# Two layers of banded products: three norm columns on GpSimd, a band copy on ScalarE alone, and a new order of operations in both layers

## The chip, the cores and the metric

The kernel runs on one NeuronCore of one Trainium2 chip. Its engines are TensorE (PE in the profile, with its weight loads as PEld), VectorE (DVE), ScalarE (ACT), GpSimd (POOL) and SyncE (SP), which issues almost all of the DMA transfers. The metric is the time of one execution in device microseconds; the profile's span is the time from the first to the last instruction, a little shorter.

## The reference

The input x is a 512 x 512 grid of 64 channels in 32-bit floating point. Two layers of the same form follow each other, each with its own weights:

```python
x = x + conv(gn(x))            # twice
# gn: group norm, 32 groups of 2 channels over the whole grid
# conv:
xn    = ln(x)                                        # over 64 channels
left  = (xn @ Wl + bl) * mask * sigmoid(xn @ Wlg + blg)   # 64 -> 128
right = (xn @ Wr + br) * mask * sigmoid(xn @ Wrg + brg)
gate  = sigmoid(xn @ Wog + bog)
out[i, j, h] = sum over d = -4..4 of left[i + d, i, h] * right[i + d, j, h]
return (ln(out) * gate) @ Wo + bo                    # 128 -> 64
```

So of `left` only a band of nine entries for each row is ever used, `right` and `gate` are needed on the whole grid, and `out` mixes nine neighbouring rows of `right` for each of the 128 hidden channels. The group norm of layer two needs sums over the whole output of layer one.

## The kernel before

The rows are cut into nine overlapping blocks of 64 (56 new rows each), the columns of a block into two chunks of 128 for each half of the grid: 18 chunks a layer. The two halves of the grid lie on the two halves of the 128 partitions. A chunk is handled in 16 steps (`NU`), each of one unit of eight columns, and the function `layer` runs over the steps. In one step t several units are in different stages, so that the engines overlap:

- Loading (`load`, `fetch`, `take_left`, `recall`; all on SP at the start of a step): z, a unit of the input; XR, the input again for the residual; A, a slab of the left band (8 slabs in a chunk, 4 transfers each, in three buffers); zg, a stored transposed unit, loaded for step t + 2 into one of two buffers.
- Input norms: `scaled` and `moved` (z times ga, plus gb; on GpSimd except early in a layer; in every fourth step also the units of the next step, "scale next" and "move next"), `inner_stats` (VectorE), `centred` and `rescaled` (GpSimd, for the unit of step t + 2), `transposed` (TensorE, for t + 1), `kept` (ScalarE copies the transposed unit to zT, SP stores it as "later").
- The right product: `right` twice (32 TensorE matmuls each for columns 0 to 3 and 4 to 7, into pairs of PSUM banks), `right_gate` (ScalarE sigmoid into sg), `right_end` (VectorE product into RO).
- The band: `mix` is one band product of eight hidden channels, A times RO (32 matmuls in two PSUM banks). A chunk has 16, in its steps 0 to 9 as 2, 1, 2, 2, 1, 2, 1, 2, 2, 1. Each leaves two halves, which are copied back into RO: "copy a" by ScalarE; "copy b" by VectorE, except that the second band's "copy b" in layer one is ScalarE's (`SECOND_ON_ACT`).
- The output norm: `out_stats` (VectorE, 3 to 7 a step), `solve` in every fourth step ("a": three small ScalarE instructions; "d": 14 small VectorE instructions that give rs and nm for both norms), `norm` (one instruction for each of eight columns into the single buffer on: columns 0 to 3, then the rest on ScalarE, and the last `NV` on GpSimd, "norm columns").
- The output: `gates` (TensorE, zg times the gate's weights), `gated` (ScalarE sigmoid), `turned` (16 TensorE transposes of on), `times_gate` (VectorE, two products into ZH), `end` (32 matmuls with Wo, for the unit of the step before; "last product" in the lists), `ended` (VectorE adds XR; SP stores two halves), and in layer one `biased` (GpSimd adds the biases to XR) and `sums` (TensorE, the group sums for layer two).

The lists `FIRST` and `SECOND` give the order in which the operations of one step are written out for layer one and layer two. Every engine runs its own instructions in exactly that order (`InOrder`), so that a list fixes five queues at once; between engines only data and buffers make an instruction wait. PSUM buffers are handed out in rotation: four single banks in layer two (three in layer one) for gates, turned, end and solve (and the band in layer two), and two pairs of banks for the right products and the transposes (and the band in layer one). A transposed unit therefore waits until VectorE has read the first right product of the same step, and the next step's first right product until VectorE has read the second.

Below, "step 0" to "step 15" are the steps of a chunk (t modulo 16): bands in 0 to 9, solves in 0, 4, 8 and 12.

Of the kernel before, what the change touches and what calls it, by code (L numbers as in the profile page):

```python
# [31 lines left out]
UP = (1024.0 / 27.0) ** 2  # L32

APART = (False, True)
NV = (1, 2)
SECOND_ON_ACT = (True, False)

FIRST = [
    ("out stats", 2), "gates", "gated", ("project", 0), ("project", 4), "turn",
    ("sigmoid", 0), ("out stats", 3), "scale", ("right", 0), ("sigmoid", 4),  # L40
    ("norm", (0, 4)), "norm columns", "centre", "move", "last product", ("right", 4),
    "times gate", "rescale", "transpose", ("out stats", 99), "inner stats", "keep", "solve",
    "end", ("band", 0), ("copy a", 0), "sums", "bias", ("band", 1), ("copy b", 0),
    ("solve on", "a"), "scale next", "move next", ("norm", (4, 8)), ("copy a", 1),
    ("solve on", "d"), ("copy b", 1),
]
SECOND = [
    ("out stats", 3), "scale", ("out stats", 2), "gates", ("project", 0), "gated",
    ("sigmoid", 0), ("project", 4), ("out stats", 99), ("right", 0), ("sigmoid", 4), "turn",
    ("norm", (0, 4)), "last product", "norm columns", "centre", "scale next", "rescale",  # L50
    "times gate", "transpose", ("band", 0), "keep", "move next", "end", ("right", 4),
    ("copy b", 0), "inner stats", "solve", "move", ("copy a", 0), ("band", 1),
    ("solve on", "a"), ("copy b", 1), ("copy a", 1), ("norm", (4, 8)), ("solve on", "d"),
]
ORDERS = (FIRST, SECOND)

# [47 lines left out]
def tile_two_banded_layers(  # L104
# [679 lines left out]
    def layer(src: bass.AP, dst: bass.AP, w: dict, stats: bool, then=None):  # L784
# [59 lines left out]
        A, sti, sto = {}, {}, None  # L844
        order, nv, second_on_act = (x[0 if stats else 1] for x in (ORDERS, NV, SECOND_ON_ACT))
        for t in range(min(loads), last_t + 3):
# [263 lines left out]
```

## Time and profile before

| | us |
|---|---|
| median of 3 runs | 4771.6 (4764.16 to 4789.46) |
| the profiled execution | 4769.15 |
| its span | 4767.2 |
| busy DVE / PE / ACT / POOL | 4007.1 / 3885.2 / 3608.6 / 3274.7 |
| busy 2700 to 4500 us (layer two's middle): DVE / PE / ACT / POOL | 1603.7 / 1557.5 / 1468.5 / 1368.6 |

Layer one's steps with output run from 510 to 2540 us, layer two's from 2793 to the end; before each, the first units are normed and the left band is made. The operations are recorded under one source line, so that groups have to be told apart by their tiles: `bank<-zg,pack` are the gate products, `banks<-pack,zT` the right products, `bank<-ident,on` the turn, `bank<-pack,ZH` the last product, `RO<-bank` a band copy, `on<-RO,rs,nm` a norm column. In a timeline a line has the start, the length and the engine of a run of equal instructions, and in brackets how long the engine was idle before it and what ended that. A wait for several things is put down to the one that came last in the profile.

### The profile page before, as it was taken

Reading aid. Unit: us, or ns where it says so; the run is one execution under the profiler, and the core shown is the slowest. Engines: PE = TensorE matmul, PEld = TensorE weight load, DVE = VectorE, ACT = ScalarE, POOL = GpSimd, SP = SyncE. Lnnn points to the kernel's source line nnn. Section 1 sums busy time; section 2 is a strip of 40 time slices with the busy share of each in tenths; the row PEclk is TensorE's granted clock in tenths of the full one; section 3 lists DMA queues with packets and bytes.
Section 4 is the critical chain, followed back from the end, with each engine's and each line's share of the span. In section 5 each row is a group of like instructions: output and inputs, shape, how many; then the busy total and the mean of one; then the engine's idle time right before and its main releaser. Section 6 shows DMA issues by size and latency. Waiting matters only on the chain. (4 is left out here: it accounts for less than half of the span.)

```text
span 4767.2 us, 193179 instructions
## 1 busy us (share of the span) xinstructions
PE 3885.2 (81%) x76306; PEld 3337.2 (70%) x76306; DVE 4007.1 (84%) x10943; ACT 3608.6 (76%) x8410; POOL 3274.7 (69%) x3427
## 2 busy tenths in 40 slices
PE   1035899999999999999985478888888888888898
PEld 0024787888787878887864467777777777777776
DVE  7864888888888888888877488988899998999898
ACT  0023888888888888898974378888888888888887
POOL 0036888888888888888723487777777777777751
PEclk9987999999999999999997799999999999999999
DMA  7958677777777777777764867777777777777776
GB/s 311 401 120 126 182 208 204 212 217 211 212 208 208 210 208 209 214 212 210 207 171 110 104 189 208 214 220 208 210 221 214 221 212 211 213 219 215 217 200 185
DMA packets 1437809, 983.48 MB, mean 206 GB/s; under 512 B 167363, under 2 KB 1284585, under 8 KB 1432553
## 3 DMA queue, kind: packets, MB, share of 16 engines
q1 hardware_dynamic: 1432064, 969.69, 74.4%
q8 instruction: 604, 9.90, 0.9%
q14 instruction: 301, 2.46, 0.2%
q10 hardware_dynamic: 4840, 1.43, 0.1%
HBM read 658.35 MB, written 312.40 MB: 204 GB/s over the span
## 5 line engine op out<-in xcount | busy, mean ns | idle before, releaser
L381 ACT ACTIVATE on<-RO,nm,rs 128x128 f32<-128x128 f32 x3744 | 1588.5, 492 | 91.8 <-DVE nm L381 44.9
L381 PEld LDWEIGHTS banks<-pack,zT 64*128 64x128 f32 x18576 | 1304.4, 203 | 380.6 <-ACT zT L381 204.4
L381 PE MATMUL banks<-pack,zT 64*128 64x128 f32 x18576 | 1350.8, 292 | 174.4 <-ACT zT L381 149.3
L381 DVE TENSOR_TENSOR RO<-banks,sg 128x512 f32<-128x512 f32 (+1 forms) x1188 | 796.3, 677 | 464.4 <-ACT sg L381 387.6
L381 POOL TENSOR_SCALAR on<-RO,rs,nm 128x128 f32<-128x128 f32 x864 | 383.9, 451 | 975.7 <-ACT sg L381 504.5
L381 ACT ACTIVATE sg<-banks 128x512 f32<-128x512 f32 (+1 forms) x1188 | 695.0, 590 | 311.1 <-PE banks L381 287.1
L381 PE MATMUL bank<-zg,pack 64*128 64x448 f32 (+1 forms) x2304 | 727.3, 615 | 213.5 <-DMA zg<-later 193.8
L381 DVE BATCH_NORM_STATS2 sto<-RO 128x6 f32<-128x256 f32 x2304 | 803.8, 412 | 0.8
L381 DVE SCALAR_TENSOR_TENSOR ZH<-bank,pack,gate 128x448 f32<-128x448 f32 (+1 forms) x1152 | 739.5, 684 | 63.0 <-ACT gate L381 34.1
L381 ACT ACTIVATE gate<-bank 128x448 f32<-128x448 f32 (+1 forms) x1152 | 563.8, 541 | 172.6 <-issue 103.0
L381 POOL TENSOR_TENSOR z<-z,ga 128x512 f32<-128x512 f32 x536 | 681.2, 1279 | 17.2 <-DMA z<-mid_x 8.7
L381 PE MATMUL bank<-pack,ZH 128*64 128x64 f32 x18432 | 667.3, 226 | 17.8 <-DVE nm L381 16.7
L381 POOL TENSOR_TENSOR z<-z,gb 128x512 f32<-128x512 f32 x536 | 677.5, 1277 | 5.1
L381 POOL TENSOR_TENSOR z<-z,rs 128x512 f32<-128x512 f32 x586 | 618.3, 1056 | 71.6 <-DVE rs L381 44.6
L381 POOL TENSOR_TENSOR z<-z,sti 128x512 f32<-128x512 f32 x586 | 624.3, 1066 | 20.8 <-DVE sti L381 20.8
L381 PEld LDWEIGHTS bank<-pack,ZH 128*64 128x64 f32 x18432 | 587.4, 138 | 60.9 <-DVE nm L381 24.2
L381 ACT ACTIVATE zT<-banks 128x512 f32<-128x512 f32 (+1 forms) x1084 | 460.1, 475 | 72.0 <-PE banks L381 62.8
L381 DVE BATCH_NORM_STATS2 sti<-z 128x6 f32<-128x128 f32 x2344 | 504.1, 282 | 0.5 <-POOL z L381 0.3
L381 PE MATMUL bank<-ident,on 64*128 64x64 f32 x9216 | 453.8, 227 | 27.5 <-ACT gate L381 25.0
L381 PEld LDWEIGHTS bank<-zg,pack 64*128 64x128 f32 x2304 | 240.5, 191 | 336.5 <-DMA zg<-later 62.7
L381 PEld LDWEIGHTS bank<-ident,on 64*128 64x128 f32 x9216 | 426.5, 141 | 69.6 <-ACT gate L381 44.7
L381 DVE TENSOR_TENSOR XR<-bank,XR 120x512 f32<-120x512 f32 (+1 forms) x576 | 390.9, 679 | 2.5 <-PE bank L381 1.2
(154 smaller groups left out, 4020.5 us busy)
## 6 DMA issues: line engine op xcount, KB each, us to landing
later<-zT SPq DMA_DIRECT2D x576, 256.0 KB
A<-left_of SPq DMA_DIRECT2D x1152, 128.0 KB
zg<-later SPq DMA_DIRECT2D x576, 256.0 KB
z<-in_x_dram SPq DMA_DIRECT2D x576, 128.0 KB
z<-mid_x SPq DMA_DIRECT2D x576, 128.0 KB
gn_x<-in_x_dram SPq DMA_DIRECT2D x16, 4096.0 KB
XR<-in_x_dram SPq DMA_DIRECT2D x448, 112.0 KB
mid_x<-XR SPq DMA_DIRECT2D x448, 112.0 KB
```

The lines of the kernel that those rows point to most:

```text
L381: return lambda *a, **k: tc.keep_in_program_order(f(*a, **k))
```

## The change

Nothing that is computed changes. In layer two `NV` goes from 2 to 3: three of the eight norm columns are GpSimd's, five ScalarE's. In layer two `SECOND_ON_ACT` becomes true: both halves of a step's second band are copied by ScalarE. Both lists are written anew:

```diff
-NV = (1, 2)
-SECOND_ON_ACT = (True, False)
+NV = (1, 3)
+SECOND_ON_ACT = (True, True)
 
 FIRST = [
-    ("out stats", 2), "gates", "gated", ("project", 0), ("project", 4), "turn",
-    ("sigmoid", 0), ("out stats", 3), "scale", ("right", 0), ("sigmoid", 4),
-    ("norm", (0, 4)), "norm columns", "centre", "move", "last product", ("right", 4),
-    "times gate", "rescale", "transpose", ("out stats", 99), "inner stats", "keep", "solve",
-    "end", ("band", 0), ("copy a", 0), "sums", "bias", ("band", 1), ("copy b", 0),
-    ("solve on", "a"), "scale next", "move next", ("norm", (4, 8)), ("copy a", 1),
-    ("solve on", "d"), ("copy b", 1),
+    ("out stats", 2), "gates", "scale", "centre", ("project", 0), "gated", "scale next",
+    ("project", 4), "turn", ("out stats", 3), ("sigmoid", 0), "rescale", "last product",
+    ("sigmoid", 4), ("out stats", 99), ("right", 0), "transpose", ("right", 4),
+    "times gate", "inner stats", "end", ("band", 0), ("norm", (0, 4)), "solve", "sums",
+    "keep", ("copy a", 0), ("solve on", "a"), ("norm", (4, 8)), "norm columns", ("band", 1),
+    "move next", ("copy b", 0), ("solve on", "d"), "move", ("copy a", 1), "bias",
+    ("copy b", 1),
 ]
 SECOND = [
-    ("out stats", 3), "scale", ("out stats", 2), "gates", ("project", 0), "gated",
-    ("sigmoid", 0), ("project", 4), ("out stats", 99), ("right", 0), ("sigmoid", 4), "turn",
-    ("norm", (0, 4)), "last product", "norm columns", "centre", "scale next", "rescale",
-    "times gate", "transpose", ("band", 0), "keep", "move next", "end", ("right", 4),
-    ("copy b", 0), "inner stats", "solve", "move", ("copy a", 0), ("band", 1),
-    ("solve on", "a"), ("copy b", 1), ("copy a", 1), ("norm", (4, 8)), ("solve on", "d"),
+    "centre", ("out stats", 3), "gates", ("project", 0), "scale", "gated", ("out stats", 2),
+    ("project", 4), "scale next", ("sigmoid", 0), "turn", ("right", 0), "times gate",
+    ("out stats", 99), ("sigmoid", 4), "rescale", "last product", "end", "transpose",
+    ("band", 0), ("band", 1), ("right", 4), ("norm", (0, 4)), "keep", ("copy b", 0),
+    ("copy a", 0), "inner stats", ("norm", (4, 8)), "norm columns", "solve", "move next",
+    "move", ("solve on", "a"), ("solve on", "d"), ("copy a", 1), ("copy b", 1),
 ]
```

Read engine by engine, this is what becomes of the queues of one step:

| queue | before | after |
|---|---|---|
| layer one, PE and ACT | | the same order |
| layer one, DVE | out stats 5, right 0, right 4, times gate, other out stats, inner stats, end, copy b 0, solve d | other out stats directly after the first five |
| layer one, POOL | scale, norm columns, centre, move, rescale, bias, scale next, move next | scale, centre, scale next, rescale, norm columns, move next, move, bias |
| layer two, PE | | the same order |
| layer two, ACT | gated, sigmoids, norm 0 to 3, keep, copy a 0, solve a, copy a 1, norm 4 and 5 | gated, sigmoids, norm 0 to 3, keep, copy a 0, norm 4, solve a, copy a 1, copy b 1 |
| layer two, DVE | all out stats, right 0, times gate, end, right 4, copy b 0, inner stats, copy b 1, solve d | out stats 5, right 0, times gate, other out stats, end, right 4, copy b 0, inner stats, solve d |
| layer two, POOL | scale, norm columns (2), centre, scale next, rescale, move next, move | centre, scale, scale next, rescale, norm columns (3), move next, move |
| both layers, SP after the loads | store of zT ("later"), stores of the output | stores of the output, store of zT |

## The prediction

> **What bounds the kernel now.** I read the page's busy shares first, then the waits of layer two's middle (2700 to 4500 us), then the timelines of TensorE, VectorE and the SP queue beside each other.
>
> ```profile
> PE 3885.2 (81%) x76306; PEld 3337.2 (70%) x76306; DVE 4007.1 (84%) x10943; ACT 3608.6 (76%) x8410; POOL 3274.7 (69%) x3427
> ```
>
> No engine is full. VectorE (DVE) leads, and it is what the change relieves; were it the bound, the change would pay. The waits say what it waits for:
>
> ```profile
> POOL on L381 <- ACT sg L381: 320.7, 148, 7.2
> DVE RO L381 <- ACT sg L381: 119.9, 80, 9.6
> PE bank L381 <- DMA zg<-later: 115.1, 57, 4.4
> PEld bank L381 <- DMA zg<-later: 59.0, 26, 4.5
> ```
>
> Columns: total us, times, longest. The last two are one cause: the gate products wait for zg, the block recalled from DRAM. The first two follow from it. TensorE and VectorE around one such wait (step 7 of a chunk):
>
> ```profile
> 3311.59 1.15 PE L381 MATMUL bank<-RO,A 64*64 64x128 f32 x32
> 3316.83 1.86 PE L381 MATMUL bank<-zg,pack 64*128 64x448 f32 x4 [4.09 <-DMA zg<-later]
> 3318.46 3.65 PE L381 MATMUL banks<-pack,zT 64*128 64x128 f32 x32
> ```
> ```profile
> 3314.59 1.39 DVE L381 BATCH_NORM_STATS2 sto<-RO 128x6 f32<-128x256 f32 x4
> 3321.13 0.69 DVE L381 TENSOR_TENSOR RO<-banks,sg 128x512 f32<-128x512 f32 x1 [5.14 <-ACT sg L381]
> ```
>
> All engines stop, and TensorE is then slow: the same four gate products take 1.02 us one step later, the projections 1.95. Why zg is late stands in the SP queue:
>
> ```profile
> 3302.74 0.55 SPq L381 DMA_DIRECT2D zg<-later  x1
> 3303.39 0.55 SPq L381 DMA_DIRECT2D later<-zT  x1
> 3304.03 1.11 SPq L381 DMA_DIRECT2D out_dram<-XR  x2
> 3305.24 3.28 SPq L381 DMA_DIRECT2D z<-mid_x  x4
> 3308.57 1.02 SPq L381 DMA_DIRECT2D XR<-mid_x  x2
> 3309.69 3.82 SPq L381 DMA_DIRECT2D A<-left_of  x4
> 3313.61 0.55 SPq L381 DMA_DIRECT2D zg<-later  x1
> 3314.26 0.55 SPq L381 DMA_DIRECT2D later<-zT  x1
> ```
>
> SP issues back to back, some 0.55 us and a gap of 0.1 for each transfer, and without waiting: 10.9 us from recall to recall, where TensorE's two-band step takes 6.8. The zg for this step was issued at 3313.61 and the product starts 3.2 us after. So SP is the bound here. Its group for a step costs about 4.7 us, and 3 to 4 more with a slab A; slabs fall in 8 of 16 steps, all in steps 1 to 11. Taking the starts of the gate products from the timeline for 14 chunks of each layer, a chunk lasts 116.4 us (layer one) and 114.0 (layer two). Steps 0 to 3 hardly vary (7.28, 7.65, 6.86, 6.83 in layer two); steps 4 to 12 vary by up to 4 us; the shortest of each step sum to 102.6 us in layer two, 110.4 in layer one. The difference, 11.4 and 6.0 us a chunk, is waiting for SP and the slow clock after it:
>
> ```profile
> 3310.00:3330.00 20.00, 15.91 (x300) 13.91 (x299) 13.41 (x32) 12.91 (x29) 13.46 (x15) 0.83 0.81 219
> 3392.00:3412.00 20.00, 19.20 (x430) 17.40 (x429) 19.70 (x52) 17.91 (x41) 17.43 (x19) 1.00 0.78 216
> ```
>
> Columns after the length: busy PE, weight loads, DVE, ACT, POOL, then granted clock (0.83 against 1.00), DMA share, GB/s. SP waits for compute again only in steps 12 to 15 (at step 13: recall issued 3366.10, next store 3370.31). A chunk is therefore SP's unbroken run from step 15 to step 12 of the next chunk, some 95 us with the landing, and about 20 us of compute in steps 12 to 15. **Compute counts only in those 20 us, in the last 140 us of the kernel, and in the filling of the layers.**
>
> **The change part by part.** The profiled execution took 4769.15 us (span 4767.2), 2.4 below the median of 4771.6; the sum is made against it. There are 18 chunks a layer; first and last overlap filling and draining, so I count 17.
>
> Layer two, second band's copy from DVE to ACT: six a chunk, 108. Starts of successive DVE instructions lie 0.60 us apart (row 683 ns), so 65 us leave DVE; on ACT the same form costs 584 ns, 0.49 apart, 53 us. The six steps are 0, 2, 3, 5, 7 and 8, all in SP's run; in steps 2 and 3 TensorE has no idle and 6.82 us of work, so it covers DVE there as well. Effect 0. If both covers were gone, -65.
>
> Layer two, third norm column: 288 leave ACT at 0.41 us (four in 1.68), 118 us, and cost GpSimd 0.43 each (two in 0.88), 124 us. GpSimd's whole step is up to two or three pairs of scale and move (1.25 each), centre and rescale (1.02 each) and the columns (1.3). In the old order the columns wait early in the step for the turn (the 320.7 us above) with all else behind them. In the new one centre, scale, scale next and rescale are done while the turn is awaited, and only the moves are queued behind. From one norm to the next I get 5.8 us (step 0 to 1), 7.05 (2 to 3), 8.3 (3 to 4, 7 to 8), 7.05 (4 to 5), against steps of 6.8 to 9.4: columns finish at most 4.3 us after the turn, and the next turn comes over 5 us after. Rescale waits for the solve's rs after steps 0, 4, 8 and 12 as before, 7 us ahead of its transposes. Effect 0; if that slack were gone, 1.5 us at the two long intervals, 17 x 3.0 = +51.
>
> Layer two, solve: ACT now does its last norm column ahead of the solve's preparation. Behind it stand the DVE roots, then next step's right product, which frees the banks of the transposes. In steps 0, 4 and 8 SP's run covers it. In step 12 nothing does: zT starts 3362.74, preparation 3363.47, DVE's first root 3364.18 after 0.67 of waiting. One column later: +0.41 x 17 = +7; 0 to +9.
>
> Layer two, stores: out (VectorE) now precedes later (zT) in SP. At steps 14 and 15 XR's sum ends about 0.4 us before zT (3375.91 plus 0.68 against about 3377.0), so SP starts its run some 0.3 earlier: -5; bounds -7 and +2.
>
> Layer one, stores: the same swap, but here the sum ends after zT (later issued at 1803.67, out at 1804.95 once XR's sum ended at 1804.9). The later store now waits behind out: about +0.45 a chunk, +8; bounds 0 and +12.
>
> Layer one, GpSimd: its column and the bias move behind rescale; the bias is last. The bias of step t-1 must be in before VectorE's sum in t; the worst is step 4 (three moves, bias): 6.5 us after its turn, where that sum comes some 10 after. Effect 0. Below: TensorE's waits put down to GpSimd's column there (19.9 and 16.6 us in 1500, 12.9 chunks) are 2.8 a chunk, and 20 of 116 us are open: -8. Above: one column's 0.45 a chunk in the open part, +8. The sixth and seventh out-stats of steps 12 and 0 move ahead of the right product, where VectorE waits 4.35 and 0.70 us anyway; 0, bounds -6 and +6.
>
> Engine orders that the lists leave as they were: TensorE in both layers, ACT in layer one.
>
> Clock: the stall at step 12 grows slightly when VectorE is quicker, so the slow clock after it is met more often. Steps 12 to 14 average 6.19, 6.77 and 5.88 us, with worst values of 7.50, 7.42 and 6.64. I take 0.3 of the 2.7 us between, +5; bounds 0 and +46.
>
> Draining of layer two: without unit loads SP is lighter, DVE busy 36.3 of 40 us in the banded part (4626 to 4666), and late steps are ACT's six columns and two gates, 3.25 us. Some of six copies (0.60) and some eight columns (0.41): -5; bounds -7 and 0. Filling: SP issues left_of stores there; 0, bounds -5 and +5.
>
> Sum: 7 - 5 + 8 + 5 - 5 = +10, so 4779 against the profiled run, 4781 on the median's footing. I say 4780.
>
> A rule against this reading: the Trainium skill, DMA: Bandwidth & Descriptors, section Issuing engines are not separate DMA queues, says that the time a sequencer takes to initiate a DMA is usually small relative to the DMA itself. The row above has SP issuing without a break while engines wait. By the rule SP would not be the bound, DVE would be, and the sum would be that of the first rival.
>
> **The rivals.** First, VectorE is the bound after all: 84% busy overall, and layer two windows of 19.70 in 20 us speak for it; the stalls of 4 us with SP continuous speak against. It gives -65 - 5 + 15 = -55, on the median's footing (as the next two) 4717. Second, the slow clock: with a shorter compute each chunk of layer two falls into the slow form of steps 12 to 14; 17 x 2.7 = 46, and the other terms +5: 4823. It decides over 24 us from 1.1 us a chunk (19 of its own). Rows for it: step 14 is either 5.0 or 6.5, the granted clock 0.80 between 3355 and 3377; against it: the stall is already long in most chunks. Third, GpSimd becomes the bound in layer two as costed: +51 + 10, 4833; that it is busy for only 1368.6 of the 1800 us from 2700 speaks against.
>
> **How the numbers follow.** Chance of the forecast (within 0.5%, 24 us, about what a measurement of this kernel can tell from no change) 0.50. VectorE rival 0.20, faster by over 0.5%. Clock 0.16, GpSimd or an unseen wait 0.14, slower. The range leaves out the lower half of the first rival and the far end of the last: 4725 to 4830; the likeliest case's own is 4760 to 4793.
>
> **What would show it.** Right: layer two's chunk near 114 us, DVE's busy time down by about 74 us (108 x 683 ns) without a shorter span; ACT's norm columns 288 fewer, GpSimd's 288 more; more DMA zg waits, SP continuous from step 15 to 12. Wrong: chunks of 110 us or less with fewer zg waits (VectorE was the bound), or SP waiting within steps 1 to 10, or TensorE's turn waiting for GpSimd's on. Wrong altogether if SP's issue time itself changes, since every chunk rests on it.

## The result and the profile after

The changed kernel takes 4740.65 us (median of 9 runs, 4736.91 to 4760.5); the kernel before, run beside it, 4771.6 (9 runs, 4750.18 to 4789.46). The ratio is 0.9948 with a 95% interval of 0.9925 to 0.9970. So the change made the kernel 0.5% faster, about 25 us (the ratio is formed from all runs; the two medians alone lie 31 us apart). The forecast was 4780, 8 us slower, which it counted as no change. The time lies inside the range given, but the sign was missed, and the interval does not reach 1. The profiled execution took 4740.65 us, its span 4738.8.

The page of the changed kernel, the busy shares and three groups (busy time, mean ns, idle time before them and its main releaser):

```profile
PE 3881.9 (82%) x76306; PEld 3333.9 (70%) x76306; DVE 3954.6 (83%) x10835; ACT 3571.5 (75%) x8230; POOL 3398.7 (72%) x3715
...
L381 POOL TENSOR_SCALAR on<-RO,rs,nm 128x128 f32<-128x128 f32 x1152 | 509.5, 453 | 607.1 <-ACT sg L381 315.1
...
L381 PE MATMUL bank<-zg,pack 64*128 64x448 f32 (+1 forms) x2304 | 722.0, 610 | 203.8 <-DMA zg<-later 173.7
...
L381 POOL TENSOR_TENSOR z<-z,rs 128x512 f32<-128x512 f32 x586 | 617.6, 1055 | 153.9 <-DVE rs L381 131.2
```

VectorE is busy 52.5 us less (4007.1 to 3954.6; the prediction had about 74), GpSimd has 288 norm columns more (864 to 1152) and 124 us more work, ScalarE 37 us less. None of it by itself makes the end come earlier, as long as TensorE still waits for zg: 203.8 us before its gate products, where the kernel before has 213.5 us (193.8 of it put down to zg). The waits of layer two's middle, 2700 to 4500 us (total us, times, longest):

```profile
POOL on L381 <- ACT sg L381: 182.7, 121, 4.7
DVE RO L381 <- ACT sg L381: 142.3, 121, 4.9
PE bank L381 <- DMA zg<-later: 112.3, 57, 4.0
...
PEld bank L381 <- DMA zg<-later: 63.4, 26, 4.2
POOL z L381 <- DVE rs L381: 47.5, 39, 2.5
```

VectorE's and GpSimd's numbers change places with their work; the two waits for zg are what they were (112.3 and 63.4 us, before 115.1 and 59.0). SP, then, is still what the step waits for. The difference is in its queue. The changed kernel's SP timeline in layer two (start, length, engine; each line a run of equal transfers):

```profile
3276.38 0.55 SPq L381 DMA_DIRECT2D zg<-later  x1
3277.03 0.82 SPq L381 DMA_DIRECT2D out_dram<-XR  x2
3277.95 0.56 SPq L381 DMA_DIRECT2D later<-zT  x1
3278.60 2.56 SPq L381 DMA_DIRECT2D z<-mid_x  x4
3281.21 1.02 SPq L381 DMA_DIRECT2D XR<-mid_x  x2
3282.33 3.25 SPq L381 DMA_DIRECT2D A<-left_of  x4
3285.68 0.55 SPq L381 DMA_DIRECT2D zg<-later  x1
3286.33 0.82 SPq L381 DMA_DIRECT2D out_dram<-XR  x2
```

These are the transfers of the rows shown of before, from one recall of zg to the next, 9.30 us where those took 10.87. Much of that difference is chance, since z and A vary from step to step. What hardly varies is the pair of output stores: 0.82 us behind zg, where it took 1.11 behind the store of zT. Over the pairs for which SP did not wait, in the middles of the two layers (700 to 2300 and 2900 to 4500 us), the median is 1.08 us before (186 and 222 pairs) and 0.82 after (172 and 171). The store of zT takes 0.55 and 0.56, but the z pair behind it takes 1.24 where it took 1.16 behind the output, so that a part of the gain is given back. All of SP's issue time together, divided by the steps, falls by 0.08 us a step in layer one and 0.13 in layer two. The prediction had taken it as fixed.

From the starts of the gate products, in the two profiled executions: layer one from its first to its last lasts 2027.4 us before and 2010.3 after, layer two 1964.9 and 1958.2, what lies between them 255.9 and 252.1. In layer two, steps 4 to 11 became 1.1 us a chunk shorter, and steps 12 to 14 became 1.0 us longer (18.84 to 19.84).

### The profile page after: what moved, and what is told of

It is laid out like the page before. It is cut to its first block, busy times and chain, and to the rows that moved or that the text cites. A ratio compares the mean times of both kernels' runs of the same rounds, so it can differ in the third digit from the quotient of the medians.

```text
span 4738.8 us, 192730 instructions
## 1 busy us (share of the span) xinstructions
PE 3881.9 (82%) x76306; PEld 3333.9 (70%) x76306; DVE 3954.6 (83%) x10835; ACT 3571.5 (75%) x8230; POOL 3398.7 (72%) x3715
## 5 line engine op out<-in xcount | busy, mean ns | idle before, releaser
L381 ACT ACTIVATE on<-RO,nm,rs 128x128 f32<-128x128 f32 x3456 | 1477.7, 493 | 92.8 <-DVE nm L381 67.0
L381 POOL TENSOR_SCALAR on<-RO,rs,nm 128x128 f32<-128x128 f32 x1152 | 509.5, 453 | 607.1 <-ACT sg L381 315.1
L381 PE MATMUL bank<-zg,pack 64*128 64x448 f32 (+1 forms) x2304 | 722.0, 610 | 203.8 <-DMA zg<-later 173.7
L381 POOL TENSOR_TENSOR z<-z,rs 128x512 f32<-128x512 f32 x586 | 617.6, 1055 | 153.9 <-DVE rs L381 131.2
```

What stands on the lines that cost most here:

```text
L381: return lambda *a, **k: tc.keep_in_program_order(f(*a, **k))
```

## The experiments

My theory after this: the swap of the stores on SP shortens SP's issue and gives the gain in both layers; layer two's later solve takes a part of it back. The rivals: layer one's new order on GpSimd and VectorE gives it; the relief of VectorE in layer two gives it; SP's issue is not the bound at all, only the DMA engines behind it. Every kernel was run beside the kernel before. That one's median was 4760.9 us beside the first four experiments, 4764.8 beside the next four, 4769.8 beside the three after them and 4755.4 beside the last, so kernels of different groups are compared by their ratios; 0.001 is 4.8 us.

| kernel | ratio to before | 95% interval |
|---|---|---|
| the change | 0.9948 | 0.9925 to 0.9970 |
| the swap of the stores alone | 0.9956 | 0.9938 to 0.9974 |
| the change without the swap | 0.9998 | 0.9982 to 1.0015 |
| the change with the solve early | 0.9896 | 0.9878 to 0.9913 |
| layer one's list alone | 0.9968 | 0.9954 to 0.9983 |
| zg recalled by ScalarE | 0.9707 | 0.9686 to 0.9728 |
| zg recalled in halves | 1.0483 | 1.0462 to 1.0503 |
| the two constants alone | 0.9989 | 0.9970 to 1.0008 |
| the orders without the constants | 0.9918 | 0.9896 to 0.9939 |
| layer one's orders, both swaps | 0.9943 | 0.9925 to 0.9961 |
| solve early in step 12 alone | 0.9919 | 0.9898 to 0.9940 |
| zT stored by ScalarE too | 0.9810 | 0.9794 to 0.9826 |
| zg recalled by ScalarE but in three steps | 0.9727 | 0.9709 to 0.9746 |

**The swap alone.** In the lists of before, only "keep" moves behind "end":

```diff
-    "times gate", "rescale", "transpose", ("out stats", 99), "inner stats", "keep", "solve",
-    "end", ("band", 0), ("copy a", 0), "sums", "bias", ("band", 1), ("copy b", 0),
+    "times gate", "rescale", "transpose", ("out stats", 99), "inner stats", "solve",
+    "end", "keep", ("band", 0), ("copy a", 0), "sums", "bias", ("band", 1), ("copy b", 0),
...
-    "times gate", "transpose", ("band", 0), "keep", "move next", "end", ("right", 4),
+    "times gate", "transpose", ("band", 0), "move next", "end", "keep", ("right", 4),
```

> The kernel before, with one thing of the change: on SP the two stores of the output come ahead of the store of zT, in both layers; all other queues as before. Theory (SP's issue is the bound and the swapped pair of stores is issued in 0.82 us where it took 1.08): SP is busy 0.09 to 0.13 us less a step, some 12 steps a chunk lie in its run, 17 chunks a layer, so -18 in layer one and -26 in layer two: 4725 to 4745 against 4771.6, and no cost of the later solve, since ScalarE's order is the old one. Rival (layer one gained by the order of GpSimd and of the output statistics): no change, 4762 to 4781. Rival (layer two's VectorE was relieved): no change either.

Measured: 4741.03 us against 4760.86, 0.9956 (-21 us). That is the theory's value, and both rivals lie outside the interval. The SP timeline of this kernel has the short pair:

```profile
3297.97 0.55 SPq L381 DMA_DIRECT2D zg<-later  x1
3298.62 0.82 SPq L381 DMA_DIRECT2D out_dram<-XR  x2
3299.53 0.55 SPq L381 DMA_DIRECT2D later<-zT  x1
```

The size can be followed too, over 14 chunks of each layer in this profiled execution and in that of before. SP's issue, with its short gaps, falls by 1.5 us a chunk in both layers. Its waits of 0.2 us and more grow by 0.8 us a chunk in both, nearly all of it in steps 13 to 15 (7.05 to 7.78 in layer one, 5.09 to 5.80 in layer two). A chunk becomes 0.8 and 0.7 us shorter, which is 25 us in 17 chunks of each layer, against 21 by the ratio. The waits can grow because the pair of stores comes later, or only because SP now arrives earlier at what it waits for; the two were not separated.

**The change without the swap.** "keep" goes back ahead of "end", with every other queue as changed:

```diff
-    "times gate", "inner stats", "end", ("band", 0), ("norm", (0, 4)), "solve", "sums",
-    "keep", ("copy a", 0), ...
+    "times gate", "inner stats", ("band", 0), ("norm", (0, 4)), "solve", "sums",
+    "keep", "end", ("copy a", 0), ...
...
-    ("out stats", 99), ("sigmoid", 4), "rescale", "last product", "end", "transpose",
-    ("band", 0), ("band", 1), ("right", 4), ("norm", (0, 4)), "keep", ("copy b", 0),
+    ("out stats", 99), ("sigmoid", 4), "rescale", "last product", "transpose",
+    ("norm", (0, 4)), "keep", "end", ("band", 0), ("band", 1), ("right", 4), ("copy b", 0),
```

> The changed kernel with the store of zT put back ahead of the stores of the output, in both layers; all other queues as changed. Theory (the order of the stores gives the gain): the pair of stores takes 1.08 us again, the gain of layer one goes (+18) and layer two keeps the later solve without the shorter run of SP: 4770 to 4790. Rivals (GpSimd's and VectorE's order, or the relief of VectorE): it stays at 4735 to 4750.

Measured: 4761.3 us, 0.9998. The whole gain is gone, as the theory has it by the ratio (the expected 4770 to 4790 stood on the median of 4771.6, where the kernel before now has 4760.9). Done alone the swap gives -21 us; taken out of the change it costs 24. So the store order makes the gain. It does not follow that the rest of the change does nothing: the experiments below find a loss of 25 us (the later solve) and a gain of about 18 (the orders) that happen to cancel here.

```profile
3302.92 0.55 SPq L381 DMA_DIRECT2D zg<-later  x1
3303.57 0.55 SPq L381 DMA_DIRECT2D later<-zT  x1
3304.22 1.14 SPq L381 DMA_DIRECT2D out_dram<-XR  x2
```

**The change with the solve early.** In layer two the solve's preparation goes back ahead of ScalarE's last norm column:

```diff
-    ("copy a", 0), "inner stats", ("norm", (4, 8)), "norm columns", "solve", "move next",
-    "move", ("solve on", "a"), ("solve on", "d"), ("copy a", 1), ("copy b", 1),
+    ("copy a", 0), "inner stats", "solve", ("solve on", "a"), ("norm", (4, 8)), "norm columns", "move next",
+    "move", ("solve on", "d"), ("copy a", 1), ("copy b", 1),
```

> The changed kernel, with layer two's preparation of the solve put ahead of ScalarE's last norm column again (as in the kernel before). Theory (SP's run got shorter, the compute of steps 12 to 14 longer by 1.0 us a chunk through the later solve and the slower clock after it): -7 (the column's 0.41 us x 17) to -17 (all of the 1.0): 4723 to 4734. Rival (the longer steps 12 to 14 have another cause, such as GpSimd's third column or the two copies on ScalarE): no change from 4740, 4735 to 4746.

Measured: 4715.89 us, 0.9896, 25 us better than the change: more than the 7 to 17 expected, and faster than both kernels. Steps 12 to 14 of layer two show how the later solve costs. Windows from the gate product of step 12 to that of step 15, the first four of the changed kernel with the solve late (after the length: busy PE, weight loads, DVE, ACT, POOL, then the granted clock, DMA share, GB/s):

```profile
2984.00:3004.19 20.19, 17.73 (x277) 15.52 (x278) 14.90 (x42) 13.53 (x32) 12.55 (x17) 0.83 0.69 195
3097.33:3114.44 17.11, 14.50 (x276) 12.62 (x278) 15.71 (x47) 13.98 (x34) 13.78 (x18) 1.00 0.73 211
3212.09:3233.29 21.20, 18.74 (x276) 16.14 (x278) 14.05 (x39) 13.51 (x32) 12.56 (x17) 0.79 0.62 178
3325.14:3343.50 18.36, 15.75 (x276) 13.78 (x278) 16.70 (x49) 13.61 (x32) 13.28 (x18) 0.91 0.74 210
```

And four of the kernel with the solve early:

```profile
2981.95:3000.25 18.30, 16.23 (x277) 14.05 (x278) 13.65 (x39) 13.50 (x32) 12.56 (x17) 0.91 0.71 195
3095.37:3115.23 19.86, 17.78 (x276) 15.41 (x278) 14.07 (x39) 13.52 (x32) 12.57 (x17) 0.83 0.72 200
...
3321.25:3337.98 16.73, 14.50 (x277) 12.63 (x278) 15.64 (x47) 13.92 (x33) 13.71 (x18) 1.00 0.79 218
3430.78:3447.49 16.71, 14.50 (x277) 12.66 (x278) 15.43 (x46) 13.90 (x33) 13.51 (x18) 1.00 0.79 219
```

At the full granted clock the stretch takes 17.1 us with the late solve and 16.7 with the early one: the 0.41 us of one norm column, as costed. The rest is the clock: 1.00 in 3 and 0.83 or 0.84 in 8 of 15 chunks with the late solve, 1.00 in 6 and 0.83 in 4 with the early one, mean length 19.64 and 18.24. How often a chunk meets the slow clock differs much between executions, though. The eight kernels in which step 12's solve is early and SP recalls zg whole have means of 18.2 to 19.5 us, the two in which it is late 19.6 and 19.9. So the direct 0.4 us is shown; that the clock then takes about as much again is what these means suggest.

**Layer one's list alone.**

```diff
-FIRST = [ ...the list of before... ]
+FIRST = [ ...the list of the change... ]
```

> Layer one's new list alone; layer two's list, columns and copies as before. Theory: layer one's gain alone, -17 in its run and -4 in the filling that follows it: 4745 to 4756, and layer two's chunks at 114.0 us. Rival (the gain is layer two's VectorE relief and what differs in layer one is chance between executions): 4765 to 4780.

Measured: 4754.52 us, 0.9968, which is -15 us by the ratio, while the medians alone differ by 6. The rival's lower end, 0.9986 by its own footing, lies just outside the interval. So layer one, its swap and its orders together, has a gain of its own, of 6 to 15 us, and the rest of the 25 is layer two's.

**zg recalled by ScalarE.** The early-solve kernel, with one transfer of each step taken off SP:

```diff
-            if t + 2 in outs:
+            if t + 2 in outs and t not in outs:
                 recall(outs[t + 2])
...
                     gated(o)
+                    if t + 2 in outs:
+                        recall(outs[t + 2], en.scalar)
```

> The kernel of the third experiment, with one transfer of each step (the recall of zg) issued by ScalarE, after its gate sigmoids, and no longer by SP; two steps ahead as before, the same bytes. Theory (SP's issue is the bound of steps 0 to 11): SP loses 0.35 to 0.55 us and a gap of 0.1 a step, some 12 steps a chunk, 34 chunks, 184 to 265 us at most; a chunk of layer two can't fall below its 102 us of shortest steps, one of layer one not below 110, and ScalarE pays 0.6 a step where it isn't covered (steps 12 to 15): so 4500 to 4640 against 4716. Rival (the DMA engines, 0.78 busy, are what makes SP's issue slow, or the wait for zg is only the landing): 4690 to 4735, and SP's own instructions get longer.

Measured: 4624.91 us, 0.9707: 91 us better than the early solve, 140 better than before, the fastest of all. TensorE's wait for zg is gone:

```profile
L381 PE MATMUL bank<-zg,pack 64*128 64x448 f32 (+1 forms) x2304 | 747.0, 601 | 19.3 <-DVE ZH L381 9.0
```

203.8 us idle before the gate products in the changed kernel, 19.3 here; a chunk lasts 112.7 us in layer one and 109.5 in layer two, where the early solve has 115.4 and 112.6. In the middles of the two layers SP now waits 182 and 188 times (gaps of 0.2 us or more; 236 and 209 us), where the changed kernel has 76 and 80 times (113 and 113 us), and about half of the waiting now lies outside steps 13 to 15. The DMA engines carry the same bytes at a share of 0.85 from 2700 to 4500 us, where the changed kernel has 0.77. So it was SP's queue, and not the DMA engines, that set the pace. Whether the time of the issue counts, or that the recall no longer stands behind z, XR and A, this run does not separate; the next one does. The Trainium skill, DMA: Bandwidth & Descriptors, section Issuing engines are not separate DMA queues, says that issuing from several engines saves only the sequencer's time, which is usually small relative to the DMA. That it saves this time agrees with the run. How long the transfers themselves take was not measured; but one issue a step, small or not, is worth 91 us here, because the issues of one queue follow each other and add up.

ScalarE's own queue shows what the move costs there:

```profile
3228.31 0.98 ACT L381 ACTIVATE gate<-bank 128x448 f32<-128x448 f32 x2
3230.64 0.33 ACTq L381 DMA_DIRECT2D zg<-later  x1
3231.07 1.09 ACT L381 ACTIVATE sg<-banks 128x512 f32<-128x512 f32 x2 [1.79 <-DMA A<-left_of]
```

The issue takes 0.33 us, but in this row it starts 1.35 us after the gate has ended, and the sigmoid behind it 1.79; the trace puts that down to a transfer of A, which neither of them uses. Of 545 issues after 700 us, 76 start more than 0.5 us after ScalarE's instruction ahead has ended; the median is 0.04. Why they are held was not tested.

**zg recalled in halves.** The changed kernel, the same bytes in two transfers of 64 partitions:

```diff
-        en.sync.dma_start(o.t, later[o.at])
+        for e in range(2):
+            en.sync.dma_start(o.t[e * S : (e + 1) * S], later[o.at][e * S : (e + 1) * S])
```

> The changed kernel with the recall of zg in two transfers of 64 partitions instead of one of 128: the same bytes and rows, one more instruction on SP in each step. Theory (SP's issue is the bound and is paid by the instruction): +0.3 to +0.65 a step, 12 steps a chunk, 34 chunks: +120 to +265, 4860 to 5005. Rival (paid by the bytes or rows, or SP not the bound): 4735 to 4760.

Measured: 4996.56 us, 1.0483: 255 us slower than the change for one more instruction a step. TensorE's wait before the gate products goes from 203.8 to 353.1 us, and SP reads:

```profile
3292.19 1.09 SPq L381 DMA_DIRECT2D zg<-later  x2
3293.38 0.97 SPq L381 DMA_DIRECT2D out_dram<-XR  x2
3294.45 0.56 SPq L381 DMA_DIRECT2D later<-zT  x1
```

The second half costs 0.60 us and a short gap, and the pair of stores behind it 0.98 in the median where it took 0.82: 0.8 us a step, and the chunks grow by 7.8 and 8.5 us, while SP's own waiting falls to 3.8 and 3.1 us a chunk, from 8.1 in both layers of the changed kernel. The recall stands where it stood and the bytes are the same, so the issue time counts; a half (0.60 us on the mean) takes no less than the whole (0.53 to 0.55), so on SP this transfer is paid by the instruction and not by the bytes.

**The two constants alone**, with the lists of before:

```diff
-NV = (1, 2)
-SECOND_ON_ACT = (True, False)
+NV = (1, 3)
+SECOND_ON_ACT = (True, True)
```

> The kernel before with the two constants alone: layer two's third norm column on GpSimd and its second band's second copy on ScalarE; both lists and SP's queue as before. The solve's preparation stays ahead of the last norm column. Theory of the prediction (both lie beside SP's run: 0): 4755 to 4767 against 4761. Rival (the relief is worth what the third experiment gained beyond the swap alone, 4716 against 4741): 4735 to 4742, and VectorE busy 55 us less.

Measured: 4759.0 us against 4764.77, 0.9989 with 1 inside the interval. The rival's 0.9945 to 0.9960 is outside the interval. Relieving VectorE is worth nothing that this shows.

**The orders without the constants**: the early-solve kernel with the diff above turned round.

> The kernel of the third experiment with the two constants put back (two norm columns on GpSimd, the second band's second copy on VectorE): the orders of all queues without the relief. If the relief makes the 25 us between the third experiment and the swap alone: 4735 to 4746. If the orders (of GpSimd and VectorE in layer two) make it: 4710 to 4722.

Measured: 4723.52 us, 0.9918. The constants' share of the early-solve kernel is then about 10 us, with overlapping intervals, and most of the 29 us between the swap alone (0.9956) and that kernel (0.9896) is made by the orders. These are those of GpSimd and VectorE in both layers and, in layer two, one of ScalarE: its last norm columns now stand ahead of the second band's copy.

**Layer one's orders, with the swap in both layers**: the kernel just named, with layer two's list of before and "keep" behind "end" in it:

```diff
-SECOND = [ ...the list of the early-solve kernel... ]
+SECOND = [ ...the list of before, "keep" behind "end"... ]
```

> Layer one's new list, and layer two's old one with nothing but the swap of the stores; the two constants as before. So against the swap alone (4741) it has layer one's new orders of GpSimd and VectorE, and against the kernel of the orders without the relief (4723.5) it lacks layer two's. If layer one's orders make the 18 us between them: 4719 to 4728. If layer two's make it: 4736 to 4746. By the single traces (layer one from its first to its last gate product: 2018.5 with the swap alone, 2010 to 2017 with the new list; layer two 1950.5 against 1941.2) about half each: 4728 to 4736.

Measured: 4741.29 us against 4769.78, 0.9943. By the ratio that is 6 us better than the swap alone and 12 worse than the orders of both layers. So layer two's orders may have the larger part, but both differences lie within overlapping intervals, and the split stays open.

**The solve early in step 12 alone.**

```diff
-            for item in order:
+            for item in TWELFTH if not stats and t % NU == 12 else order:
```

TWELFTH is layer two's list of the early-solve kernel.

> The changed kernel with layer two's preparation of the solve ahead of the last norm column in steps 12 alone; in steps 0, 4 and 8 behind it, as changed. Theory (only steps 12 to 15 are not covered by SP's run, and there the later solve also brings the slower clock): the whole gain of the third experiment, 4711 to 4722. Rival (each of the four solves of a chunk costs alike): a quarter to a third of the 25 us, 4731 to 4736.

Measured: 4725.66 us, 0.9919: 14 of the 25 us. That is between what the two views expected (the change 0.9948, all four solves early 0.9896), with intervals that touch both ends. Step 12 makes about half; whether steps 0, 4 and 8 make the rest is not settled.

**zT stored by ScalarE too.**

```diff
-            en.sync.dma_start(later[u.at], u.t[:, :, :P])
+            en.scalar.dma_start(later[u.at], u.t[:, :, :P])
```

> The kernel that recalls zg from ScalarE, with the store of zT issued by ScalarE as well, directly after it has written zT; SP is left with the loads and the stores of the output. If SP is still the bound there: it loses another 0.65 us a step, and chunks go towards the sums of the shortest steps (110 and 103 us, from 112.7 and 109.5): 4560 to 4610 against 4625. If ScalarE's issue of 0.55 us a step in the open steps 12 to 15 (4 x 0.6 x 34 = 80) and its later stages weigh as much: 4620 to 4680. If SP is no longer the bound there: 4620 or above too.

Measured: 4678.24 us, 0.9810: 49 us worse than with the recall alone. The first expectation, 4560 to 4610, is excluded. ScalarE's queue in layer one:

```profile
1295.22 0.86 ACT L381 ACTIVATE zT<-banks 128x512 f32<-128x512 f32 x2
1295.84 0.53 ACTq L381 DMA_DIRECT2D later<-zT  x1
1296.42 0.91 ACT L381 ACTIVATE on<-RO,nm,rs 128x128 f32<-128x128 f32 x2 [0.34 <-ACT zT L381]
```

The norm column doesn't follow right behind the write of zT but after 0.34 us of idle time, which the trace puts down to zT; I read it as the store in between waiting for ScalarE's own write. From 700 to 2300 us such waits are 21.4 us ahead of norm columns and 18.7 ahead of band copies, 2.9 us a chunk, and a chunk of layer one goes from 112.7 to 115.0 us. That ScalarE pays more than SP gains fits these rows; it was not tested apart.

**zg recalled by ScalarE, but in steps 12 to 14 by SP**, where SP waits anyway:

```diff
-            if t + 2 in outs and t not in outs:
+            if t + 2 in outs and (t not in outs or t % NU in (12, 13, 14)):
                 recall(outs[t + 2])
...
-                    if t + 2 in outs:
+                    if t + 2 in outs and t % NU not in (12, 13, 14):
                         recall(outs[t + 2], en.scalar)
```

> The kernel that recalls zg from ScalarE, with the recalls written out in steps 12, 13 and 14 given back to SP. Theory (a chunk is SP's run from step 15 to 12 and the compute of the steps between, where SP waits and every instruction of ScalarE counts): SP takes the three in the time it waits there anyway (4.5 us in step 14, 2 in step 13 in the kernel that recalls from ScalarE), ScalarE is rid of 3 x 0.55 us a chunk in the open steps, 56 us over 34 chunks if all of it lies on the path: ratio to the kernel before 0.959 to 0.967, where the recall from ScalarE in all steps had 0.9707 (4568 to 4607 on a footing of 4765). Rival (ScalarE's issue lies beside its waits there, and the gain is only in steps 0 to 11): 0.969 to 0.973. A third way (SP, given these three, starts its next run later by 0.6 us a chunk): 0.974 or above.

Measured: 4628.18 us against 4755.39, 0.9727 (0.9709 to 0.9746), where the recall in all steps has 0.9707. My theory's 0.959 to 0.967 is excluded: taking ScalarE's three issues out of those steps does not shorten the chunk. Whether they were not on the path, or SP's later start took back what they gave, can't be told apart.

## Why the prediction was wrong

**What bounds the kernel** was read rightly in the main. SP runs almost without a break from step 15 to step 12 and waits for compute in the steps between. In six profiles with zg recalled whole by SP (before, the change, the swap alone, the change without it, the early solve, the orders without the constants) its waits of 0.2 us and more lie for the most part in steps 13 to 15: 5.2 of 6.0 us a chunk in layer two before, 6.9 of 8.1 after. One transfer off SP gives 91 us, one more costs 255. That compute counts only in those 20 us of a chunk is not confirmed: the orders below are worth 18 us that nothing here places in these steps.

**The step that failed is the pair of store terms**, "Layer two, stores ... -5" and "Layer one, stores ... +8". I asked only when the stores become ready, and took SP's issue time as the same in any order. The runs show -21 us for the two together (swap alone) and -24 (swap undone). SP's waits in steps 13 to 15 do grow, by 0.7 us a chunk in layer one, where I had put +0.45, and by as much in layer two, where I had expected an earlier start of 0.3 (a part may be only SP's earlier arrival). What I had left at nothing is larger: the pair is issued 0.26 us faster when it stands behind zg and not behind the store of zT, and SP's issue becomes 1.5 us shorter a chunk. The prediction's last sentence named this, "Wrong altogether if SP's issue time itself changes", and gave it no chance. The rows to see it were in the trace of before: zg took 0.35 us behind XR and 0.55 behind A in the median, so an issue time depended on what stood ahead of it. The prediction's rows show zg behind A; this is one behind XR, from the same trace:

```profile
3375.14 1.03 SPq L381 DMA_DIRECT2D XR<-mid_x  x2
3376.27 0.35 SPq L381 DMA_DIRECT2D zg<-later  x1
```

**Solve and clock**, +7 and +5, had the right sign and mechanism, and were too small: 25 us in all. The column's 0.4 us a chunk is measured as costed; that the slower clock behind it was more than the 0.3 us taken is what the means of steps 12 to 14 suggest. Step 12 comes to about 14 us, near the 12 forecast; the claim that steps 0, 4 and 8 are covered by SP's run is not confirmed. The second rival, the slow clock in every chunk of layer two, did not come: steps 12 to 14 grew by 1.0 us a chunk and not by 2.7.

**Copies and norm columns**, 0 and 0, fit the runs: alone they give 0.9989, with 1 inside the interval. The first rival (VectorE as the bound, -55) falls with the same run. So does the third: GpSimd's 124 us more cost nothing that the runs show, though it waits longer for rs ahead of its rescale (153.9 us in the changed kernel, 71.6 before).

**The orders of GpSimd and VectorE**, 0 with bounds of 8 and 6 us either way in layer one and without a term of their own in layer two, are worth about -18 together with ScalarE's norm columns ahead of its copy in layer two, which had no term either (0.9918 against 0.9956, intervals that just overlap). The forecast missed it; which instruction makes it was not found.

The terms as measured, stores -21, solve +25, orders -18, constants -5 to -10, add up to -19 to -24, against -25 measured for the whole. That the total of the change equals the swap's own gain is chance: the other terms nearly cancel. Draining and filling were not measured by themselves.

## What to carry to other kernels

Where one engine issues transfers back to back and others wait for the last of them, count its instructions and not its bytes: here one transfer of 0.5 us a step on another queue was worth more than any reordering, and cutting one in two cost five percent. Give the issue time of each transfer by what stands ahead of it, and cost a swap in such a queue by that as well as by when the data is ready. Before a relief of the busiest engine is counted as a gain, or an added wait as covered, find the steps in which the bound engine itself waits, and test the others: the later solve and the orders counted for more than this rule gave.

## What the hardware showed unexpectedly

The issue time of the same transfer depends on the transfer ahead of it in the queue. The pair of output stores, in the medians of these kernels: 0.82 us behind zg and 0.83 behind XR, 0.98 behind zg in two halves, 0.99 to 1.03 behind A, 1.08 behind the store of zT. zg: 0.35 behind XR and 0.55 behind A, and 0.33 on ScalarE's queue. What makes the difference was not tested.

The granted clock in steps 12 to 14 came in levels, not in a spread: about 16.7 us at 1.00, 18.3 at 0.91, 19.5 to 20.0 at 0.83 to 0.85 and 20.5 or more at 0.78 to 0.80 in layer two of the kernels with the early solve and SP's recall, with the same instructions. The levels are counts: from 2900 to 4500 us the clock record of the changed kernel's trace holds only 1.0 and 0.5, and the 0.5 in pieces of 3.41 us or, three times, 6.83. One piece in 18.3 us makes 0.91, two in 19.8 make 0.83.
